# A graph layer's mean over neighbours: three sorted lanes instead of four, and keys fetched four blocks at a time

## The chip, the cores and the metric

The kernel runs on one core of a Trainium2 chip. Its engines work side by side, each through its own list of instructions in order: PE (TensorE, matrix products), DVE (VectorE), ACT (ScalarE), POOL (GpSimd, which here also issues the indirect DMAs) and SP (SyncE, which issues most plain DMAs). The time is device microseconds of one execution. A profile is one execution taken by the hardware profiler; its times are counted from the first instruction.

## The reference

```python
h = jnp.maximum(_layernorm(x, axis=-1), 0.0)
local = features[tgt]            # features = h, 100000 nodes x 64
nbr = features[src]              # 3300000 edges, sorted by tgt
x = jnp.concatenate([local, nbr - local], axis=-1)
y = jnp.einsum('ec,oc->eo', x, W) + b
s = jax.ops.segment_sum(y, tgt, num_segments=num_v)
cnt = jax.ops.segment_sum(jnp.ones((y.shape[0],), y.dtype), tgt, num_segments=num_v)
return jnp.where(cnt > 0, s / jnp.maximum(cnt, 1.0), 0.0)      # added to x
```

The layer is linear, so what costs is one sum: for each node, the rows of `h` of all its neighbours. Every node has itself as a neighbour, and about 32 others, spread over all 100,000 nodes.

## The kernel before

**Beginning.** The normalized rows are written to HBM, each as three bf16 parts whose sum is the row, with a column of ones (`h3`, 194 columns). Edges come sorted by target. Most of them are dealt out in windows of 8064 (8192 less a padding of 128), whose targets lie within 256 nodes; four windows are a quad, and a lane is the 128 partitions that hold up to 32 quads, one window a partition. There are 100 quads in lanes of 32, 32, 32 and 4. The edges that are left go in chunks of 3584 (`chunks`): one indirect DMA on POOL fetches a row of `h` for each of 128 edges, 28 of them make a chunk, and PE sums the rows with a matrix of zeros and ones that DVE makes (`hot`, L362).

**Sort** (`sort_lane`). Each partition sorts its 8192 keys by source with a bitonic network: a copy of one side (`tmp`, L481 on ACT in the first lane, L486 on POOL in the others) and a minimum and a maximum on DVE (L476, L477), with `held` letting the next copy go ahead of a compare. Sorted keys go to `ksort` in HBM. The 100,000 sources are cut into 157 blocks of 640; counts on ACT and DVE (L567, L623) tell where each block's keys begin.

**Fill** (`fill_lane`). For groups of eight blocks, `fetch` gathers 64 keys from each block's beginning with one indirect DMA per block (L672, 161 a lane). DVE splits them into source within the block and target within the window, and the results go through HBM (`sr_d`, `dt_d`) to where quads load them. Keys that fit in no block's 64 slots are spill: DVE finds up to 64 of them a window with one instruction each (L745), and one indirect DMA each fetches them (L758).

**Main part** (`quads`). A block of a quad is a "pick": `gh` (three tensor-scalar compares on DVE for eight blocks, L845) selects rows of a table of `h` by six matmuls (L873), ACT casts the result (`gs`, L875), and `dh` (a compare on DVE for four blocks, L362) sums them into the targets by sixteen small matmuls (L886). 32 blocks stay in SBUF as tables, so each lane goes over its quads in five passes of 32, 32, 32, 32 and 29 picks a quad. At the end of a quad's pass ACT copies the sums out of PSUM (L910), and in passes 1 to 4 POOL adds those of the passes before (L912). In the last pass two indirect DMAs per quad fetch spill rows (L826), and DVE then adds the nodes' own rows and joins the three parts (L919, L923, L925); SP stores the result (L342 to L345).

**Order.** Instructions are issued in the order of the Python program, which weaves its parts by an account. The sort of lane 0 runs alone with `chunks`, `own_part` and the writing of tables beside it: each step of the sort yields a number of ns, and one row gather is issued for every GATHER ns of that account. Then the fill of lane 0 makes four groups, `drain(ev)` issues the gathers that are left, and the main part begins. Beside it `background` yields the rest of the fill, the sort of the next lane and so on, in steps booked at 2.083 ns an element and 290 ns for a compare, and 480 ns for a step of the fill; each pick allows SORT ns of it. `begin`, called two groups of four blocks ahead, issues the loads of a quad; `put` issues its sums and, in the last pass, its end on DVE. `add_later` and `add_now` hand stores to SP some picks later. After the last quad come the chunks' and windows' shared rows and the last stage, the product with the weights.

The account as it stands:

```python
spent = 0.0
for _ in quads():
    spent -= SORT
    while spent <= 0:
        with pinned(last["hots"].ins):
            spent += next(rest, SORT)
```

## Time and profile before

| | before |
|---|---|
| median of 3 runs | 19243.74 us (19207.14 to 19248.48) |
| the profiled execution | 19284.92 us, its span 19283.3 us |
| first row gather, last row gather on POOL | 347 us, 1472.5 us |
| first cast of the main part | 1767.9 us |
| last cast of the main part | 18908.2 us |
| busy: PE, DVE, ACT, POOL | 82%, 76%, 48%, 24% of the span |
| mean granted TensorE clock | 0.913 of full speed |

The busy shares are averages over stages with different limits. A row of a stage names the stretch in us, its length, each engine's busy time in it with the number of instructions in brackets, the granted clock, the mean busy share of the DMA engines and the GB/s that they moved. A row of a group names line, engine, operation, what is written and read, shapes and count, then busy us and mean ns of one, then the idle time ahead of it and what ended it. A row of waits names who waited for whom, the us in total, how often, and the longest.

### The profile page before, as it was taken

The numbers are of one execution on the slowest core, as the hardware profiler recorded it, in microseconds if no ns is written. First come the engines' busy times: TensorE is split into PE (matmuls) and PEld (weight loads), VectorE is DVE, ScalarE is ACT, GpSimd is POOL, SyncE is SP. The second block draws the span as 40 slices with busy tenths as digits, with TensorE's granted clock in tenths as the row PEclk, the third lists the DMA queues.
The fourth block names the chain that finished last, engine by engine and source line by source line (L and its number), as shares of the span: only waits on it lengthen the run. The fifth ranks groups of instructions, "written<-read, shape, count | busy, mean of one in ns | idle before, by whom it ended". The sixth has DMA issues, their size and how long they took to land. (4 is left out here: it accounts for less than half of the span.)

```text
span 19283.3 us, 796285 instructions
## 1 busy us (share of the span) xinstructions
PE 15795.1 (82%) x356735; PEld 13909.3 (72%) x356735; DVE 14736.7 (76%) x17616; ACT 9286.0 (48%) x19353; POOL 4620.4 (24%) x3293
## 2 busy tenths in 40 slices
PE   0342699999998768999998877889999887898896
PEld 0332588888886557888887756778888775787785
DVE  6667579999987667899998656888889865566664
ACT  3334355555555334555556433445555643554452
POOL 6442202222222321112222231221122223111104
PEclk9556899999998789999999888999999988999998
DMA  7862334444444434344444444343344433344456
GB/s 276 121 114 75 79 115 138 126 141 127 142 122 124 101 88 119 104 132 126 143 127 134 116 101 122 100 114 104 124 121 142 118 107 102 113 134 112 121 184 238
DMA packets 1520611, 2432.07 MB, mean 126 GB/s; under 512 B 905304, under 2 KB 1113699, under 8 KB 1511011
## 3 DMA queue, kind: packets, MB, share of 16 engines
q1 hardware_dynamic: 1327762, 2081.35, 36.8%
q10 hardware_dynamic: 134086, 239.08, 4.7%
q0 software_dynamic: 55328, 60.66, 2.2%
q8 instruction: 2788, 45.68, 1.0%
q14 instruction: 647, 5.30, 0.1%
HBM read 1836.50 MB, written 583.01 MB: 125 GB/s over the span
## 5 line engine op out<-in xcount | busy, mean ns | idle before, releaser
L875 ACT CAST gs<-gp 128x386 bf16<-128x386 f32 x15700 | 7444.5, 487 | 7775.7 <-PE gp L873 7102.8
L873 PE MATMUL gp<-tab,gh 128*128 128x193 bf16 x94200 | 9142.7, 252 | 1303.1 <-ACT gs L875 460.8
L873 PEld LDWEIGHTS <-gh 128*128 128x128 bf16 x94200 | 7997.5, 99 | 2161.8 <-issue 1585.4
L886 PE MATMUL total<-gs,dh 32*128 32x193 bf16 x251200 | 6487.4, 247 | 890.1 <-issue 679.9
L886 PEld LDWEIGHTS <-dh 32*128 32x128 bf16 x251200 | 5298.9, 94 | 1823.6 <-issue 1518.4
L362 DVE TENSOR_TENSOR dh<-dt,c 128x2048 bf16<-128x2048 int16 (+1 forms) x4000 | 4737.5, 1193 | 2300.9 <-PE total L886 1771.9
L845 DVE TENSOR_SCALAR gh<-srs,pcols 128x2048 bf16<-128x2048 int16 (+1 forms) x6000 | 4976.2, 875 | 1133.4 <-PE gp L873 957.0
L486 POOL COPY tmp<-keys 128x1024 f32<-128x1024 f32 (+13 forms) x1017 | 1242.3, 1222 | 7265.2 <-DVE keys L477 6980.3
L912 POOL TENSOR_TENSOR whole<-whole,prev 128x1544 f32<-128x1544 f32 x400 | 1323.0, 3308 | 2809.9 <-ACT whole L910 2274.8
L477 DVE TENSOR_TENSOR keys<-tmp,keys 128x1024 f32<-128x1024 f32 (+10 forms) x1356 | 1838.1, 1361 | 29.3 <-issue 1.0
L476 DVE TENSOR_TENSOR keys<-tmp,keys 128x1024 f32<-128x1024 f32 (+10 forms) x1356 | 1573.4, 1165 | 315.0 <-ACT tmp L481 254.2
L910 ACT COPY whole<-total 128x386 f32<-128x386 f32 (+1 forms) x2000 | 817.4, 496 | 528.0 <-PE total L886 456.3
L672 POOL DMA_INDIRECT kf<-ksort,at_i x644 | 632.6, 982 | 1433.8 <-ACT k L713 850.1
L405 POOL DMA_INDIRECT nb<-h,si x588 | 562.3, 956 | 595.8 <-PE ps L410 283.2
L826 POOL DMA_INDIRECT rows_x<-h,xs x200 | 194.9, 975 | 1941.7 <-PE total L886 1312.4
L481 ACT COPY tmp<-keys 128x1024 f32<-128x1024 f32 (+9 forms) x339 | 338.1, 1002 | 421.5 <-issue 188.3
L994 PEld LDWEIGHTS o_ps<-w_own,hT 128*128 128x128 f32 x784 | 182.4, 287 | 445.4 <-ACT hT L988 339.3
L919 DVE SCALAR_TENSOR_TENSOR whole<-own,whole 128x193 f32<-128x193 bf16 x800 | 297.8, 413 | 138.6 <-POOL whole L912 114.6
L410 PE MATMUL ps<-nb,hot 128*128 128x193 bf16 x588 | 89.6, 327 | 361.6 <-DVE sums L423 168.3
L994 PE MATMUL o_ps<-w_own,hT 128*128 128x128 f32 x784 | 230.5, 427 | 183.5 <-ACT hT L988 136.7
L986 PE MATMUL t_ps<-ident,ht 128*128 128x128 f32 x392 | 93.3, 377 | 313.4 <-DVE keys L461 311.3
L410 PEld LDWEIGHTS <-hot 128*128 128x128 bf16 x588 | 74.2, 131 | 377.0 <-DVE sums L423 142.4
(189 smaller groups left out, 4437.9 us busy)
## 6 DMA issues: line engine op xcount, KB each, us to landing
srs<-sr_d SPq DMA_DIRECT2D x1900, 512.0 KB
part_d<-whole SPq DMA_DIRECT2D x400, 772.0 KB
prev<-part_d SPq DMA_DIRECT2D x400, 772.0 KB
tab<-tables ACTq DMA_DIRECT2D x148, 970.0 KB
ht<-hb SPq DMA_DIRECT2D x56, 896.0 KB
own<-h SPq DMA_DIRECT2D x400, 97.0 KB
tables<-h ACTq DMA_DIRECT2D x157, 242.5 KB
h<-parts SPq DMA_DIRECT2D x28, 1358.0 KB
```

Of the source, the lines that this page charges most:

```text
L362: return nc.vector.tensor_tensor(out.rearrange("p k (a d) -> p k a d", d=D), numbers[:, :, None].to_broadcast(shape), upto[:shape[0], :n]. ...
L405: last[POOL] = nc.gpsimd.indirect_dma_start(out=nb[:, j], out_offset=None, in_=h3, in_offset=bass.IndirectOffsetOnAxis(ap=si[:, u, at:at + ...
L476: nc.vector.tensor_tensor(lo, tmp, hi, ALU.min)
L477: last[DVE] = nc.vector.tensor_tensor(hi, tmp, hi, ALU.max)
L486: nc.gpsimd.tensor_copy(tmp, lo)
L672: last[POOL] = nc.gpsimd.indirect_dma_start(out=kf[:, c], out_offset=None, in_=ksort, in_offset=bass.IndirectOffsetOnAxis(ap=at_i[:, c0 + ...
L845: nc.vector.tensor_scalar(gh[:, b, :n].rearrange("p c i s -> p (c i s)"), srs[q, s // SL][:, :n].rearrange("p c i s -> p (c i s)"), pcols[ ...
L873: nc.tensor.matmul(gp[:, i], lhsT=ghots[q, s][:, b, i], rhs=row[:, b + i * (NB - NR), :CE], start=b == 0, stop=b == NR - 1)
L875: nc.scalar.copy(gs[q, s], gp)
L886: nc.tensor.matmul(total[:, i, to(b)], lhsT=hot[at, b * P:b * P + P], rhs=of[at], start=flags.get("start", False) and b == 0, stop=flags.g ...
L910: nc.scalar.copy(whole[:, i, :width], total[:, i, :width])
L912: nc.gpsimd.tensor_tensor(whole[:, :, :NT * CE], whole[:, :, :NT * CE], prevs.pop(q), ALU.add)
```

## The change

- Lanes: three of 32 quads instead of four; the padding of a window is 64 instead of 128, so a window has 8128 edges. More edges are left for the chunks. GATHER goes from 1250 to 900.
- Sort of lane 0: the compare is held back by one exchange, as in the other lanes.
- Fetch: one indirect DMA brings 320 consecutive keys from the beginning of the first of four blocks (41 a lane instead of 161). A new function, `apart_keys`, moves each of the other three blocks' keys to its place on DVE, by the bits of its distance: for each of eight bits one predicated copy. Each lane's keys in `ksort` are followed by end marks, since a fetch can run on.
- Spill: 48 slots are searched and fetched instead of 64.
- The end of a quad in the last pass is queued six picks after `put` (REST), in one go for its four windows, into one tile with two buffers; the load of the own rows comes eight picks later in the quad than before.
- SORT is 255 in the first four passes and 60 in the last; a step of the fill is booked at 500 ns.

```diff
-QUADS = 32, 32, 32, 4
+QUADS = 32, 32, 32
 LANES = len(QUADS)
 KG = 16
 JH = 14
 LAG = 3
-GATHER = 1250
-SORT = 240
+GATHER = 900
+SORT = 255, 255, 255, 255, 60
+REST = 6
 GAP = 5
 DUE = 10
 JA = 16
...
 NX = 2
-SPILL = NX * KS
-PAD = 128
+SLOTS = NX * KS
+SPILL = 48
+JOIN = 4
+BITS = 8
+FETCH = 320
+PAD = 64
 D = 4
 BIAS = 0x30000000
 END = 0x3A000000
-PIECES = 1024, 1024, 1024, 1024
+PIECES = 1024, 1024, 1024
 HEAD = 10
 COUNTS = 1
 GAIN = 2.0 ** 40
...
-    ksort = dram.tile([NL * P * WL + NT * P, 1], I32, name="ksort")
+    LONG = P * WL + NT * P
+    ksort = dram.tile([NL * LONG, 1], I32, name="ksort")
     sr_d = dram.tile([SETS, NCB, 2, P], I16, name="sr_d")
     dt_d = dram.tile([NG, P, SETS, SL * 2 * D], I16, name="dt_d")
...
             def exchange(lo, hi, tmp, *of):
+                if held and any(a < y and x < z for a, z in of for x, y in held[0][3]):
+                    compare()
                 if l == 0:
                     last[ACT] = nc.scalar.copy(tmp, lo)
-                    held.append((lo, hi, tmp, of))
-                    return compare()
-                if held and any(a < y and x < z for a, z in of for x, y in held[0][3]):
-                    compare()
-                nc.gpsimd.tensor_copy(tmp, lo)
+                else:
+                    nc.gpsimd.tensor_copy(tmp, lo)
                 compare()
                 held.append((lo, hi, tmp, of))
 
...
             row = few.tile([P, 1], F32, name="row", bufs=LANES)
-            nc.gpsimd.iota(row, pattern=[[0, 1]], base=l * P * WL, channel_multiplier=WL,
+            nc.gpsimd.iota(row, pattern=[[0, 1]], base=l * LONG, channel_multiplier=WL,
                            allow_small_or_imprecise_dtypes=True)
             at_i = few.tile([P, NCB + NO // 2], I32, name="at_i", bufs=LANES)
...
             nc.gpsimd.iota(first, pattern=[[CS, NCB]], base=BIAS >> 10, channel_multiplier=0)
+            off = piece.tile([P, NG * SL], I32, name="off", bufs=1)
+            nc.vector.memset(off.bitcast(F32), 0.0)
+            whole = NCB // JOIN * JOIN
+            joined = at_i[:, :whole].rearrange("p (h j) -> p h j", j=JOIN)
+            nc.vector.tensor_tensor(off[:, :whole].rearrange("p (h j) -> p h j", j=JOIN), joined,
+                                    joined[:, :, 0:1].to_broadcast([P, whole // JOIN, JOIN]), ALU.subtract)
+            bits = piece.tile([P, BITS, NG * SL], I32, name="bits", bufs=1)
+            for i in range(BITS):
+                nc.vector.tensor_scalar(bits[:, i], off, i, 1, op0=ALU.logical_shift_right, op1=ALU.bitwise_and)
             fetched = {}
 
+            def apart_keys(k, kf):
+
+                m = min(SL, NCB - k * SL)
+                n = m // JOIN
+                moved = piece.tile([P, SL // JOIN, JOIN - 1, FETCH], I32, name="moved", bufs=1)
+                of = kf[:, :n, None, :]
+                for i in reversed(range(BITS)):
+                    w = KW + (1 << i) - 1
+                    shape = [P, n, JOIN - 1, w]
+                    at = 1 << i
+                    if i == BITS - 1:
+                        nc.vector.tensor_copy(moved[:, :n, :, :w], of[:, :, :, :w].to_broadcast(shape))
+                        src = of[:, :, :, at:at + w].to_broadcast(shape)
+                    else:
+                        src = moved[:, :n, :, at:at + w]
+                    mask = bits[:, i, k * SL:k * SL + n * JOIN].rearrange("p (h j) -> p h j", j=JOIN)[:, :, 1:, None]
+                    nc.vector.copy_predicated(moved[:, :n, :, :w], mask.to_broadcast(shape), src)
+                    if i in (6, 4, 2):
+                        yield
+                keys = piece.tile([P, SL, KW], I32, name="keys", bufs=1)
+                to = keys[:, :n * JOIN].rearrange("p (h j) s -> p h j s", j=JOIN)
+                nc.vector.tensor_copy(to[:, :, 0], kf[:, :n, :KW])
+                if m % JOIN:
+                    nc.vector.tensor_copy(keys[:, n * JOIN], kf[:, n, :KW])
+                nc.vector.tensor_copy(to[:, :, 1:], moved[:, :n, :, :KW])
+                fetched[k] = keys
+                yield
+
             def fetch(k):
-                c0, m = (k * SL, min(SL, NCB - k * SL)) if k < NG else (NCB, NO // 2)
-                fetched[k] = kf = piece.tile([P, SL, KW], I32, name="kf", bufs=3)
-                for c in range(m):
+                fetched[k] = kf = piece.tile([P, SL // JOIN, FETCH], I32, name="kf", bufs=3)
+                starts = range(k * SL, min(k * SL + SL, NCB), JOIN) if k < NG else [NCB]
+                for h, c in enumerate(starts):
                     last[POOL] = nc.gpsimd.indirect_dma_start(
-                        out=kf[:, c], out_offset=None, in_=ksort,
-                        in_offset=bass.IndirectOffsetOnAxis(ap=at_i[:, c0 + c:c0 + c + 1], axis=0))
+                        out=kf[:, h, :NO * KS if k == NG else FETCH if c + JOIN <= NCB else KW], out_offset=None, in_=ksort,
+                        in_offset=bass.IndirectOffsetOnAxis(ap=at_i[:, c:c + 1], axis=0))
                     took()
                     yield
 
...
                 m = min(SL, NCB - c0)
+                yield from apart_keys(k, fetched[k])
                 kf = fetched.pop(k)[:, :m]
                 sr = piece.tile([P, SL, KW], I32, name="sr", bufs=1)[:, :m]
                 nc.vector.tensor_scalar(sr, kf, 10, None, op0=ALU.logical_shift_right)
...
 
-            kf = fetched.pop(NG)[:, :NO // 2]
+            kf = fetched.pop(NG)[:, 0, :NO * KS].rearrange("p (c s) -> p c s", s=KW)
             nc.vector.tensor_scalar(kf, kf, 10, None, op0=ALU.logical_shift_right)
             nc.vector.tensor_scalar(kf, kf, float(-(BIAS >> 10) - NCB * CS), float(2 * CS), op0=ALU.add, op1=ALU.min)
...
-            xpos = piece.tile([P, SPILL], F32, name="xpos", bufs=1)
+            xpos = piece.tile([P, SLOTS], F32, name="xpos", bufs=1)
             for s in range(SPILL):
                 nc.vector.scalar_tensor_tensor(more, over, float(s), fit, op0=ALU.is_le, op1=ALU.mult,
                                                accum_out=xpos[:, s:s + 1])
                 if s % 8 == 7:
                     yield
-            nc.vector.tensor_add(xpos, xpos, iota[:, :SPILL])
+            nc.vector.memset(xpos[:, SPILL:], 0.0)
+            nc.vector.tensor_add(xpos, xpos, iota[:, :SLOTS])
             nc.vector.tensor_scalar(xpos, xpos, row, None, op0=ALU.add)
-            xin = piece.tile([P, SPILL], F32, name="xin", bufs=1)
+            xin = piece.tile([P, SLOTS], F32, name="xin", bufs=1)
             nc.vector.tensor_scalar(xin, xno, -1.0, 1.0, op0=ALU.mult, op1=ALU.add)
             nc.vector.tensor_mul(xpos, xpos, xin)
-            xat = piece.tile([P, SPILL], I32, name="xat", bufs=1)
+            xat = piece.tile([P, SLOTS], I32, name="xat", bufs=1)
...
-                if k == 3 * GP:
+                if k == 5 * GP:
                     owns[q] = load.tile([P, W, NT, CT], BF16, name="own", bufs=1)
                     for i in range(W):
                         at = number(wb_r[0:1, 0, q * W + i:q * W + i + 1], SP, V)
...
                     return
+                closing.append((count[0] + REST, q, whole))
+
+            def close(q, whole):
+                sums = load.tile([P, W, NT, C1], F32, name="wsums", bufs=2)
                 for i in range(W):
                     for b in range(NT):
                         part = whole[:, i, b * CE:b * CE + CE]
                         nc.vector.scalar_tensor_tensor(part, owns[q][:, i, b, :CE], whole[:, i, NT * CE + b:NT * CE + b + 1],
                                                        part, op0=ALU.mult, op1=ALU.add)
                     both = whole[:, i, :NT * CE].rearrange("p (b c) -> p b c", b=NT)
-                    sums = load.tile([P, NT, C1], F32, name="wsums", bufs=6)
-                    nc.vector.tensor_reduce(sums[:, :, :C], both[:, :, :C3].rearrange("p b (s c) -> p b c s", s=3),
+                    nc.vector.tensor_reduce(sums[:, i, :, :C], both[:, :, :C3].rearrange("p b (s c) -> p b c s", s=3),
                                             axis=AX.X, op=ALU.add)
-                    nc.vector.tensor_copy(sums[:, :, C:], both[:, :, C3:])
-
-                    def addition(w=q * W + i, sums=sums):
+                nc.vector.tensor_copy(sums[:, :, :, C:],
+                                      whole[:, :, :NT * CE].rearrange("p w (b c) -> p w b c", b=NT)[:, :, :, C3:])
+                for i in range(W):
+                    def addition(w=q * W + i, i=i):
                         if w < SETS * W - 1:
-                            store(wb_r[0:1, 0, w:w + 1], slice(w, w + 1), [sums[:, b] for b in range(NT)])
+                            store(wb_r[0:1, 0, w:w + 1], slice(w, w + 1), [sums[:, i, b] for b in range(NT)])
                             return
                         at = number(wb_r[0:1, 0, w:w + 1], POOL, V)
-                        nc.gpsimd.dma_start(acc[ds(at, CH)].rearrange("(b p) c -> p b c", p=P), sums, accum_op=ALU.add)
+                        nc.gpsimd.dma_start(acc[ds(at, CH)].rearrange("(b p) c -> p b c", p=P), sums[:, i], accum_op=ALU.add)
 
                     add_later(DUE, addition)
 
...
-                    yield
+                for x in picks(g + 1):
+                    yield x
                     count[0] += 1
+                    while closing and closing[0][0] <= count[0]:
+                        close(*closing.pop(0)[1:])
                     add_now()
                 _, x, q, of = groups[g]
                 for s in of:
                     put(x, q, s)
+            for of in closing:
+                close(*of[1:])
 
         slots = {}
         filled = [0] * NL
...
                     for _ in fill_lane(l, fill, took):
-                        yield 2 * SORT
+                        yield 500
 
         with tc.tile_pool(name="keys", bufs=1) as big, tc.tile_pool(name="piece", bufs=2) as piece, \
...
             spent = 0.0
-            for _ in quads():
-                spent -= SORT
+            for x in quads():
+                spent -= SORT[x]
                 while spent <= 0:
                     with pinned(last["hots"].ins):
-                        spent += next(rest, SORT)
+                        spent += next(rest, 500)
             assert next(rest, None) is None
             add_now(True)
 
```

29 lines of the change are left out of this document (14 added, 15 removed).

## The prediction

> **What bounds the kernel now.** I read the page first, then the busy time of each stage, and only then the waits of single stages.
>
> ```profile
> span 19283.3 us, 796285 instructions
> PE 15795.1 (82%) x356735; PEld 13909.3 (72%) x356735; DVE 14736.7 (76%) x17616; ACT 9286.0 (48%) x19353; POOL 4620.4 (24%) x3293
> ```
>
> PE leads, but an average says little here. One ScalarE cast (`gs`, L875) closes each block ("pick"), so casts per stretch give the speed of the main part. The stretches below are its passes: lane 0 passes 0, 1+2, 3, 4; lane 1 the same; lane 2 pass 0, then passes 1 to 3 together, then 4; last, all of lane 3. Columns: stretch, length, ACT busy (casts), granted clock, DMA share, GB/s.
>
> ```profile
> 1768.00:2994.00 1226.00, 482.78 (x1024) 0.90 0.36 103
> 2994.00:4939.00 1945.00, 974.91 (x2049) 1.00 0.46 134
> 4939.00:5981.00 1042.00, 485.15 (x1024) 0.98 0.44 130
> 5981.00:7448.00 1467.00, 437.01 (x929) 0.82 0.41 101
> 7448.00:8398.00 950.00, 486.93 (x1024) 0.99 0.36 113
> 8398.00:10345.00 1947.00, 974.40 (x2049) 1.00 0.46 134
> 10345.00:11709.00 1364.00, 480.97 (x1025) 0.86 0.42 114
> 11709.00:12913.00 1204.00, 439.81 (x928) 0.90 0.42 108
> 12913.00:13863.00 950.00, 487.59 (x1024) 0.99 0.36 113
> 13863.00:17221.00 3358.00, 1456.55 (x3072) 0.94 0.41 120
> 17221.00:18286.00 1065.00, 440.63 (x931) 0.95 0.45 115
> 18286.00:18909.00 623.00, 297.67 (x628) 0.99 0.53 167
> 16440.00:17221.00 781.00, 382.45 (x804) 0.99 0.45 132
> ```
>
> A pick costs 0.925 us in a first pass (950/1024), 0.95 in passes 1 and 2 beside a sort, 0.97 with neither sort nor fill (the last row); there the clock is whole and PE sets the pace. The losses are at the ends of lanes: 1467, 1364, 1204 and 1065 us where about 930 to 980 would do. Two things lie there. One is the fill (`fill_lane`) and its gathers:
>
> ```profile
> 10820.00:11420.00 600.00, 457.60 (x8983) 378.06 (x8981) 325.39 (x467) 249.67 (x494) 197.60 (x176) 0.82 0.41 108
> 11507.00:11602.00 95.00, 24.04 (x253) 13.95 (x244) 11.15 (x17) 5.10 (x11) 64.33 (x65) 0.55 0.12 29
> L672 POOL DMA_INDIRECT kf<-ksort,at_i x157: 940/944/1292, 10819.3 to 11400.3; - x157
> ```
>
> (Columns: PE, PEld, DVE, ACT, POOL busy.) Twenty-two matmuls make a pick, so the first stretch, with 157 fetches, did 8983/22 = 408 picks in 600 us: 1.47 us each. The second holds the 64 single-key gathers of L758 in a row: 11 picks in 95 us. A long row of indirect DMAs on POOL stops PE, about 85/64 = 1.33 us for each; no engine is busy there but POOL. The other thing is the quad's end on VectorE (L919 to L925) in a last pass, seen alone in lane 2, where no background is left. First DVE's groups of 17221 to 18286, then who made PE wait there.
>
> ```profile
> L362 DVE TENSOR_TENSOR dh<-dt,c 128x2048 bf16<-128x2048 int16 (+1 forms) x257 | 286.4, 1117 | 285.3 <-DMA dt<-dt_d 150.9 <-PE total L886 95.7 <-PE gp L873 38.8
> L845 DVE TENSOR_SCALAR gh<-srs,pcols 128x2048 bf16<-128x2048 int16 (+1 forms) x387 | 272.7, 747 | 47.0 <-PE gp L873 47.0
> L919 DVE SCALAR_TENSOR_TENSOR whole<-own,whole 128x193 f32<-128x193 bf16 x248 | 92.0, 411 | 0.0
> L923 DVE TENSOR_REDUCE wsums<-whole 128x128 f32<-128x384 f32 x124 | 72.9, 588 | 0.0
> L925 DVE COPY wsums<-whole 128x2 f32<-128x2 f32 x124 | 19.4, 156 | 0.0
> ```
>
> ```profile
> PE gp L873 <- DVE gh L845: 93.2, 45, 4.0
> ```
>
> The end is 184.3 us over 31 quads, 6 us each, in one piece ahead of the next `gh`; PE waits 93 us for `gh`, 3 us a quad.
>
> **The change, part by part.** I sum against the profiled execution (1768 to the first cast, 17141 of main part, 375 of tail, 1.6 outside the span: 19284.9); the median of the runs is 41 us lower.
>
> *Three lanes.* Lane 3's 623 us go, and with them its sort and fill beside lane 2 (passes 1 to 3). Lane 2 then has no background: 0.925 x 1024 + 0.97 x 3072 = 947 + 2980.
>
> *More chunks.* 3,300,000 edges less 384 windows of 8128 leave 178,848: 50 chunks of 3584 instead of 21, 1400 row gathers instead of 588, all before the main part. Their price is the start-to-start time on POOL:
>
> ```profile
> 361.10 0.94 POOL L405 DMA_INDIRECT nb<-h,si  x1 [0.30 <-issue]
> 362.35 0.94 POOL L405 DMA_INDIRECT nb<-h,si  x1 [0.30 <-issue]
> 347.00:1473.00 1126.00, 399.25 (x2099) 329.89 (x2099) 703.73 (x717) 368.32 (x494) 561.72 (x588) 0.62 0.72 127
> 1473.00:1690.00 217.00, 8.61 (x56) 7.51 (x56) 208.28 (x298) 136.75 (x243) 0.48 (x1) 0.52 0.05 20
> 350.00:450.00 100.00, 9.02 (x32) 3.71 (x32) 43.53 (x72) 2.15 (x2) 75.10 (x78) 1.00 0.79 258
> 1350.00:1450.00 100.00, 13.92 (x84) 12.08 (x84) 99.04 (x97) 41.17 (x42) 68.35 (x73) 0.52 0.21 37
> L672 POOL DMA_INDIRECT kf<-ksort,at_i x644: 938/944/2325, 1691.9 to 16250.4; - x161
> ```
>
> So 1.25 us each. Until now the sort of lane 0 set this stage (fetches can start at 1692, gathers ended at 1473). The sort books 894 us (my sum over the numbers it yields); at 900 ns a gather 994 are woven into it, 406 are left. Woven in, the old pace of 1126/588 = 1.91 us becomes 1.91 x 0.9/1.25 = 1.38, above 1.25: hidden, but tight. In the first 100 us 77 gathers become 107 x 1.25 = 134 (+34); from 1350 to 1690, where `own_part` is over, 72 per 100 us become 100 x 1.25 = 125 (340 us, +80, less some waiting: 66). The sort ends near 1790. The 406 and the 10 fetches now needed follow with nothing beside them that POOL waits for: 520 us, to 2310, and 20 more to the first cast: 2330, **+562**. Bounds: POOL never idle from 347, 347 + 1410 x 1.25 = 2110 (+10 to the cast); above, if the sort is slowed by a third of what the woven gathers add (994 x 1.25 x 0.28 x 1/3, 116 us), 2450. SP gets 29 more stores of sums; their cover is the same stage. The other order in `exchange` of lane 0 holds the compare back one step, as the other lanes do; the copies keep their buffers, so I book nothing.
>
> *Keys four blocks per fetch.* Eight fetches a group become two: POOL's row of 10 us, which starved PE, becomes 2.5, and two gathers in a row I book at nothing for PE (if they stopped it as the long rows do, 2 x 1.33 us in each of 60 groups, 160 in all). In their place DVE gets eight predicated copies of 6 x (64 + 2^i - 1) elements, 4554 in all, and copies of 1658. The trace has predicated copies of other sizes, and an int32 pass of 512:
>
> ```profile
> L464 DVE COPY_PREDICATED s<-own,q 128x512 int32<-128x512 int32 x60 | 44.3, 738 | 8.4 <-remote 3.3 <-issue 2.8 <-DVE q L463 1.0
> L701 DVE COPY_PREDICATED kf<-far,kf 128x256 int32<-128x256 int32 x76 | 36.9, 485 | 0.0
> L694 DVE TENSOR_SCALAR sr<-kf 128x512 int32<-128x512 int32 x76 | 31.9, 420 | 27.2 <-issue 15.5 <-DMA kf<-ksort,at_i 11.8
> L362 DVE TENSOR_TENSOR dh<-dt,c 128x2048 bf16<-128x2048 int16 x3900 | 4696.2, 1213 | 2278.2 <-PE total L886 1749.2 <-remote 230.2 <-DMA dt<-dt_d 217.5
> L745 DVE SCALAR_TENSOR_TENSOR more<-over,fit 128x314 f32<-128x314 f32 x256 | 124.2, 485 | 6.8
> L745 DVE DVE_READ_ACCUMULATOR more<-over,fit 128x1 f32 x256 | 21.2, 83 | 0.0
> L438 DVE TENSOR_REDUCE wb<-keys 128x1 f32<-128x8064 int32 x4 | 34.2, 8553 | 68.2 <-DMA keys<-in_dst_w 68.2
> L623 DVE TENSOR_SCALAR_CACHE_REDUCE junk<-keys 128x534 bf16<-128x534 f32 x152 | 106.9, 704 | 2.0
> ```
>
> From 485 and 738: 0.99 ns an element and 0.23 fixed, 4.5 + 1.9 = 6.4 us; copies at 0.82 ns, 1.3: 7.7 us a group. Bounds: nothing if DVE's idle time took it all, twice that if broadcast operands run at half rate; I take the middle, the shapes being alike. The fill's old DVE work is (325.4 - 408 x 0.583)/18 = 4.9 us a group, 0.583 being three `gh` (747) and two `dh` (1213) per eight picks. A group books nine steps of 500, 4.5 us, which is 17.6 picks at 255 and 75 at 60. At 255 DVE needs 17.6 x 0.583 + 12.6 = 22.9 us for 17.6 picks: 1.30 us a pick, **DVE becomes the bound of the fill**, 6.6 us lost per group. Before, (600 - 408 x 0.925)/18.4 = 12.1. By the account 16 groups fall into lane 0's first pass, 11 into its pass 3, 9 into pass 4 at 60 (covered, 20 us in all), and lane 2's 20 into lane 1's pass 3. The scan of 48 spill steps (L745, 0.57 us each, 27 us against twelve picks' time of which DVE needs 7) costs 23 us, the 48 gathers 48 x 1.33 = 64 where they run in a row (lane 0's first pass), 50 between the quads' additions of a pass 3, little in pass 4.
>
> The Trainium skill, "SBUF — State Buffer", section "SBUF: two separate sides", speaks against this part: an fp32 copy within SBUF on VectorE locks GpSimd out, so a DMA issued there takes about 3.1 us instead of 0.62. By it the two fetches of a group would cost an estimated 4 us more; the fill's rows show 944 ns at the median beside such DVE work.
>
> *Pace.* 255 instead of 240 beside a sort is 6% more sort, on a DVE that is 92% busy beside one:
>
> ```profile
> 8500.00:9300.00 800.00, 774.53 (x18494) 692.24 (x18493) 738.97 (x701) 438.85 (x945) 192.95 (x113) 1.00 0.45 128
> ```
>
> Of its 739 us 249 are not one-hots (840 picks at 0.583); 6% of them are 15, two in a hundred of the stretch, most of it idle time. I take 0.956 for 0.950.
>
> *The end six picks later, 60 in the last pass.* Behind two more `dh` and the next eight blocks' `gh`, the 6 us run when PE has about two groups of four in hand (7 us): the 93 us go. DVE holds 743 us of the rows above over 32 quads, 23 each and one `eh`, against PE's 29 x 0.925 = 27 and the end's small matmuls. A last pass becomes 1065 - 93 - about 40 of lower clock = 930, and 950 in lane 0 with nine groups beside it. The own rows' load is queued two groups later on SP, behind the end that must free `own`; both move together, so the `srs` and `dt` loads behind it see the same wait.
>
> *The sum.* Lane 0: 947 + 16 x 6.6 + 23 + 64 + 27 (a sort's start, unchanged: the two reductions of 8.55 us and part of the 17 us that their load is waited for) = 1166; 2048 x 0.956 = 1957; 979 + 50 (VectorE's 70 counts at 0.70 in one piece, unchanged) + 73 = 1102; 950. Lane 1: 983; 1959; 979 + 50 + 132 + 23 + 50 = 1234; 930. Lane 2: 947 + 2980 + 930. Together 5175 + 5106 + 4857 = 15138 against 17141: -2003. With +562: 19284.9 - 1441 = 17844, less 41: **17,800**.
>
> **Rivals.** *The gathers hide* (12%): the sort loses nothing and POOL stays full to 2120: 17,590. For it: POOL is idle half of 347 to 1473; against: 406 gathers have no sort left. *DVE takes the fill in its idle time* (6%): -47 x 6.6: 17,490; against it the 92%. *The masks run at half rate* (11%): 47 x 7.7 more: 18,160. *The late end buys nothing* (10%), because `gh` is late for another reason (its `srs` load, or the `dt` that DVE waited 151 us for): three last passes at 1065, 18,205. *Fetches wait for VectorE* (2%): each at the longest time seen, 2325 ns, 47 x 2.8 = 130: 17,930; this is what the skill's page would make of it, and the median speaks against it. *Slower* (3%): the predicated copies with a stride-zero mask cost not 0.99 but over 7.7 ns an element. Then the 47 groups at full pace take 31 us more each, 1441 in all, and at 8.5 ns it ends near 19,400. No row shows such a rate; the two at hand are both near 1.
>
> **How the numbers follow.** The forecast has 56%, its own range 17,600 to 18,000. With the rivals next to it the range is 17,450 to 18,250. A measurement of this kernel tells about 0.2% (its runs lie 19207 to 19248) from no change; every case but the last is far beyond it: faster 0.96, same 0.01, slower 0.03.
>
> **What would show it.** First cast near 2330 with POOL nearly full from 1400 on; lane 2's passes near 0.93 and 0.97 a pick; a fill with DVE above 95% and about 1.3 us a pick, no stretch where only POOL is busy in pass 3 of 157 fetches; last passes near 930 with PE's wait on `gh` gone. A first cast before 2150 or after 2450, or last passes above 1000, would prove the step wrong.

## The result and the profile after

The changed kernel takes 18557.48 us (median of four runs, 18551 to 18577); the kernel before takes 19235.75 beside it. The ratio is 0.9651, interval 0.9634 to 0.9668: 678 us faster, where 17,800 was forecast, outside the range of 17,450 to 18,250. The profiled execution is 18577.3, its span 18575.7. The engines' line of its page:

```profile
PE 15064.2 (81%) x343411; PEld 13353.6 (72%) x343411; DVE 13652.2 (73%) x16240; ACT 8851.9 (48%) x18429; POOL 4303.4 (23%) x3101
```

The busy time of each stage, lane 0's passes 0, 1+2 and 4; lane 1's 1+2, 3 and 4; lane 2's pass 0, its passes 1 to 3 and its pass 4. The last row is a piece of lane 1's pass 3 in which the fill runs. (Columns: stretch, length, PE, PEld, DVE, ACT, POOL busy with instructions, granted clock, DMA share, GB/s.)

```profile
2574.00:3738.00 1164.00, 992.02 (x22415) 873.62 (x22417) 949.11 (x1325) 566.98 (x1182) 136.70 (x128) 0.92 0.37 110
3738.00:5688.00 1950.00, 1886.28 (x45081) 1688.90 (x45077) 1847.37 (x1739) 1069.87 (x2305) 494.01 (x292) 1.00 0.46 134
6808.00:8008.00 1200.00, 965.61 (x22985) 840.59 (x22986) 860.59 (x1415) 510.50 (x1077) 221.44 (x153) 0.90 0.42 109
8987.00:10933.00 1946.00, 1884.26 (x45040) 1687.93 (x45032) 1830.50 (x1732) 1070.04 (x2304) 482.69 (x289) 1.00 0.46 134
10933.00:12210.00 1277.00, 1032.56 (x22544) 899.98 (x22536) 1013.28 (x1470) 640.13 (x1369) 235.85 (x153) 0.90 0.44 122
12210.00:13297.00 1087.00, 945.75 (x23003) 832.10 (x22992) 714.47 (x1078) 489.41 (x1056) 161.46 (x94) 0.93 0.41 113
13297.00:14244.00 947.00, 934.08 (x22544) 841.71 (x22545) 571.62 (x651) 534.76 (x1152) 5.10 (x3) 0.99 0.35 113
14244.00:17142.00 2898.00, 2817.10 (x67580) 2527.21 (x67572) 1879.56 (x1921) 1604.78 (x3456) 302.54 (x95) 1.00 0.45 135
17142.00:18201.00 1059.00, 930.53 (x22928) 819.25 (x22920) 706.40 (x1070) 489.32 (x1056) 159.57 (x92) 0.95 0.40 108
11455.00:11890.00 435.00, 328.09 (x6691) 280.89 (x6693) 389.09 (x589) 194.35 (x374) 71.49 (x47) 0.86 0.45 123
```

Against the forecast's terms: first cast 2574 for 2330 (+244); lane 0's last pass 1200 for 950 (+250), lane 1's 1087 for 930 (+157), lane 2's 1059 for 930 (+129); lane 1's pass 3 1277 for 1234 (+43); lane 2's passes 1 to 3 2898 for 2980 (-82). The others are within 18. The sum is +733, which is the whole miss. Lane 2's last pass took 1065 before, some 24 of it in its last quad, where lane 3 began (1.93 us a pick, 1.11 now): the late end bought it nothing.

Two stages stand out by their waits. First that of lane 0's sort (347 to 2070), then lane 2's last pass (17142 to 18201; SPq is SP's own queue). Columns: who waits, for whom, us in total, times, longest.

```profile
ACT tmp L489 <- issue: 264.9, 78, 41.5
```

```profile
DVE dh L368 <- DMA dt<-dt_d: 207.4, 26, 11.9
PE gp L917 <- DVE gh L889: 110.7, 55, 3.8
...
SPq L348 <- DMA acc<-wsums: 301.1, 120, 3.5
SPq L351 <- DMA acc<-wsums: 74.9, 76, 2.6
```

In the first, ACT's copies for the sort stand up to 41.5 us at "issue", waiting for nothing that the profile shows. In the second, DVE waits for `dt` and PE for `gh` as before. SP stands 376 us at the stores of window sums, each of which waits for the store before it to land.

### The profile page after: what moved, and what is told of

Same layout as the page of the kernel before. It is cut to its first block, busy times and chain, and to the rows that moved or that the text cites. A ratio compares the mean times of both kernels' runs of the same rounds, so it can differ in the third digit from the quotient of the medians.

```text
span 18575.7 us, 764868 instructions
## 1 busy us (share of the span) xinstructions
PE 15064.2 (81%) x343411; PEld 13353.6 (72%) x343411; DVE 13652.2 (73%) x16240; ACT 8851.9 (48%) x18429; POOL 4303.4 (23%) x3101
## 5 line engine op out<-in xcount | busy, mean ns | idle before, releaser
L919 ACT CAST gs<-gp 128x386 bf16<-128x386 f32 x15072 | 7152.7, 487 | 7033.2 <-PE gp L917 6204.4
L917 PE MATMUL gp<-tab,gh 128*128 128x193 bf16 x90432 | 8669.7, 250 | 805.7 <-ACT gs L919 357.1
L917 PEld LDWEIGHTS <-gh 128*128 128x128 bf16 x90432 | 7603.4, 99 | 1593.2 <-issue 1065.4
L930 PE MATMUL total<-gs,dh 32*128 32x193 bf16 x241152 | 6082.0, 246 | 509.0 <-issue 315.6
L930 PEld LDWEIGHTS <-dh 32*128 32x128 bf16 x241152 | 5043.4, 94 | 1305.5 <-issue 1057.3
L889 DVE TENSOR_SCALAR gh<-srs,pcols 128x2048 bf16<-128x2048 int16 (+1 forms) x5760 | 4694.0, 861 | 1043.4 <-PE gp L917 1027.0
L491 POOL COPY tmp<-keys 128x1024 f32<-128x1024 f32 (+11 forms) x678 | 828.4, 1223 | 4588.4 <-DVE keys L483 4311.6
L482 DVE TENSOR_TENSOR keys<-tmp,keys 128x1024 f32<-128x1024 f32 (+13 forms) x1017 | 1189.1, 1176 | 501.8 <-ACT tmp L489 322.3
L411 POOL DMA_INDIRECT nb<-h,si x1400 | 1339.8, 957 | 856.8 <-issue 437.2
L483 DVE TENSOR_TENSOR keys<-tmp,keys 128x1024 f32<-128x1024 f32 (+13 forms) x1017 | 1360.6, 1346 | 20.4 <-DVE q L469 1.0
L713 POOL DMA_INDIRECT kf<-ksort,at_i x123 | 134.0, 1089 | 912.6 <-DVE keys L702 782.8
```

What stands on the lines that cost most here:

```text
L411: last[POOL] = nc.gpsimd.indirect_dma_start(out=nb[:, j], out_offset=None, in_=h3, in_offset=bass.IndirectOffsetOnAxis(ap=si[:, u, at:at + ...
L482: nc.vector.tensor_tensor(lo, tmp, hi, ALU.min)
L483: last[DVE] = nc.vector.tensor_tensor(hi, tmp, hi, ALU.max)
L491: nc.gpsimd.tensor_copy(tmp, lo)
L889: nc.vector.tensor_scalar(gh[:, b, :n].rearrange("p c i s -> p (c i s)"), srs[q, s // SL][:, :n].rearrange("p c i s -> p (c i s)"), pcols[ ...
L917: nc.tensor.matmul(gp[:, i], lhsT=ghots[q, s][:, b, i], rhs=row[:, b + i * (NB - NR), :CE], start=b == 0, stop=b == NR - 1)
```

## Experiments

### The first stage: what a row gather costs the sort

The theories: the forecast's (woven gathers hide until POOL is full); that gathers hold up the other engines; that chunk work in the in-order engines does; and that lane 0's new exchange order does.

**No weaving.** `-GATHER = 900` `+GATHER = 10 ** 9`

> One constant of the changed kernel, GATHER, from 900 to 10**9: no row gather is woven into lane 0's sort, all 1400 follow it. In the changed kernel the sort ended at 2069 (the first fetch of keys) with 994 woven, before at 1692 with 588. Forecast's theory (the sort goes at its own pace, a woven gather costs it nothing or a third of what POOL adds): sort end 1650 to 1700, first cast near 1690 + 1400 x 1.25 + 33 = 3470. Rival (each woven gather stops the sort's engines for about (2069 - 1692)/(994 - 588) = 0.93 us): 2069 - 994 x 0.93 = 1145, but DVE alone has some 910 us of work from 347 on, so 1260 to 1350; first cast near 3080. Second rival (the other order in lane 0's exchange slows the sort): sort end near 2000, first cast near 3800. In the stretch of the sort DVE should then be above 0.85 busy by the first rival only.

**Gathers alone.** The loop of `chunks` without its one-hot, matmuls, sums and stores:

```
-                    with behind():
-                        one_hot(hot, near[:, u, part * JH:part * JH + JH], P)
...
-                    before = (hot, nb, part, q)
+                    before = None
```

> Leaves out of the chunks' part the one-hot, the matmuls, the sums and their stores; the 1400 row gathers stay, 994 of them woven into the sort as in the changed kernel. If the gathers themselves hold up the other engines: the sort still ends at 1920 to 2070, and while POOL issues gathers back to back DVE and ACT stand still although nothing in the sort waits for the gathers. If the sort was held up by its in-order engines waiting for chunk work (hot for PE, ps for the sums): 1690 or earlier. The main part is not touched: last passes as in the changed kernel (1200, 1087, 1059).

**Chunks without gathers.** Matmuls read one tile of zeros: `+nb = still`, and the indirect DMA is removed.

> The counterpart: the row gathers are left out (the matmuls read one tile of zeros), and the chunks' one-hots, matmuls, sums and stores stay, in the same places of the program. If the gathers hold up the engines: the sort ends at 1400 or earlier with DVE above 0.85 busy. If the chunk work holds it up: 1900 or later. First cast soon after the sort's end, since only the last 406 places of chunk work without a gather are left.

**Gathers with a long pause**, on gathers alone: `+last[POOL] = nc.gpsimd.memset(still, 0.0)` with `still` 128x1400, ordered behind each gather and ahead of the next.

> As the run with the gathers alone (chunk one-hots, matmuls, sums and stores left out, 1400 row gathers kept), with one POOL memset of 128x1400 floats behind every gather, about 1.25 us, which needs nothing and is needed by nothing. Gathers alone, the sort ended at 2909 and did nearly nothing while POOL issued every 1.25 to 1.4 us. If it is the unbroken row of gathers that stops the other engines: gathers come every 2.5 us and last to about 3850, and yet the sort ends at 1750 or earlier, DVE being busy between 500 and 1500 as without any gather (70 to 95 us in 100). If each gather takes a fixed time from the others, whatever lies between: half the time is left to them, the sort ends near 347 + 2 x (1474 - 347) = 2600.

The stretch 500 to 1400 (columns as above) in four kernels, in this order: changed; gathers alone; with pauses; chunks without gathers.

```profile
500.00:1400.00 900.00, 342.76 (x1836) 285.38 (x1836) 477.47 (x461) 278.89 (x386) 485.14 (x513) 0.58 0.72 121
```

```profile
500.00:1400.00 900.00, 71.82 (x295) 57.08 (x294) 108.65 (x97) 72.04 (x92) 680.62 (x648) 0.50 0.30 54
```

```profile
500.00:1400.00 900.00, 290.62 (x1398) 235.54 (x1395) 715.09 (x642) 405.68 (x535) 839.27 (x754) 0.55 0.73 115
```

```profile
500.00:1400.00 900.00, 353.10 (x2092) 299.37 (x2091) 774.15 (x760) 410.30 (x556) 0.00 (x0) 0.62 0.63 93
```

The 87 counts on ACT that end the sort (min/median/max ns, first to last start), for the three experiments in the same order (chunks without gathers last):

```profile
L569 ACT ACTIVATE junk<-keys,bound x87: 501/742/743, 2822.9 to 2906.3; 128x536 bf16<-128x536 f32 x58, 128x430 bf16<-128x430 f32 x22, 128x258 bf16<-128x258 f32 x7
```

```profile
L571 ACT ACTIVATE junk<-keys,bound x87: 501/742/743, 1370.7 to 1453.9; 128x536 bf16<-128x536 f32 x58, 128x430 bf16<-128x430 f32 x22, 128x258 bf16<-128x258 f32 x7
```

```profile
L573 ACT ACTIVATE junk<-keys,bound x87: 500/742/743, 1390.8 to 1474.3; 128x536 bf16<-128x536 f32 x58, 128x430 bf16<-128x430 f32 x22, 128x258 bf16<-128x258 f32 x7
```

Without gathers the sort ends at 1474, with one every 2.39 us (the median; its memset takes 1.28) at 1454. With POOL left to issue as fast as it can, one every 1.25 us, it ends at 2906, and DVE is busy 109 us of 900, with nothing else of the chunks' work there. The unbroken row is the cause; whether the break between two gathers counts or their rate, which it halves, is not separated. Chunk work and the exchange order are not the cause: the run without gathers keeps both. One stop and its end, in the timeline of the gathers alone (start, duration, engine; in brackets the idle time before):

```profile
1585.96 1.22 DVE L480 TENSOR_TENSOR keys<-tmp,keys 128x1024 f32<-128x1024 f32 x1
...
1598.49 0.95 POOL L408 DMA_INDIRECT nb<-h,si  x1 [0.30 <-issue]
1599.45 0.37 ACT L1045 COPY own<-o_ps 128x256 f32<-128x256 f32 x1 [14.78 <-remote]
...
1599.88 0.27 PE L1042 MATMUL o_ps<-b,ones 96*128 96x128 bf16 x1 [13.78 <-issue]
1600.77 1.22 DVE L479 TENSOR_TENSOR keys<-tmp,keys 128x1024 f32<-128x1024 f32 x1 [13.59 <-issue]
```

DVE, ACT and PE stop together for some 14 us, while POOL issues every 1.25, and go on together.

My rival's figure of 0.93 us a gather was no constant. Without weaving the sort ended at 2640 instead of 1260 to 1350 and the first cast came at 2695: POOL ran the gathers ahead all the same, 1400 between 346 and 2518, since nothing in its list held them back. It also failed for the gathers alone, which ended 840 us later than its upper figure: with no chunk work, nothing breaks the row. What the changed kernel loses depends on how often POOL has to wait.

**A short pause** behind each gather of the complete kernel, as above with `still` 128x28.

> The changed kernel, complete, with a POOL memset of 128x28 floats (0.15 us for 128x56 bf16 in the stage ahead) behind each of the 1400 row gathers. If a short break is enough for the others to go on: the sort ends near 1700 to 1850 instead of 2069, and the first cast comes near that + 400 x 1.45 = 2300 to 2400. If it is POOL's share of time that counts: sort unchanged near 2069, the row behind it 10% longer, first cast 2620 to 2680.

The sort ended at 1980 instead of 2021, the first cast came at 2597 instead of 2574, the whole took 18575.6. But the memset made no break in the row:

```profile
2199.67 0.95 POOL L413 DMA_INDIRECT nb<-h,si  x1 [0.17 <-issue]
2200.61 0.15 POOL L417 MEMSET still<- 128x28 f32 x1
2200.93 0.95 POOL L413 DMA_INDIRECT nb<-h,si  x1 [0.17 <-issue]
```

It falls into the 0.30 us that POOL stands idle ahead of each gather anyway, and the gathers come every 1.25 us (the median) as in the changed kernel. So the run says nothing of a short break. How far apart gathers must be, between 1.25 and 2.39 us, was not tried.

### The last passes

**The end at once.** `-closing.append((count[0] + REST, q, whole))` `+close(q, whole)`

> The changed kernel with the quad's end on VectorE queued where it was before (directly behind the copies of the sums), nothing else undone. Forecast's theory (the end's 6 us ahead of gh are what PE waits for, 93 us a last pass): the three last passes become about 93 us longer each, 1290, 1180 and 1150, the kernel 18830. Rival on record (the late end buys nothing, gh is late for another reason): last passes 1200, 1087 and 1059 within 20 each, the kernel within 60 of 18557.

18556.4, with last passes of 1181, 1085 and 1067. The waits of its lane 2's last pass:

```profile
DVE dh L368 <- DMA dt<-dt_d: 208.5, 51, 6.3
...
PE gp L917 <- DVE gh L889: 114.0, 57, 3.8
```

The same totals as with the late end, in twice as many waits for `dt`. The six picks of delay move the wait, and do not shorten it.

**No window stores** into `acc` in the last passes (`if len(tiles) == 1:` ahead of them).

> The changed kernel without the two stores of each window's sums into acc in the last passes (the one shared row is still stored; the chunks' stores stay). In the changed kernel SP's queue waited 301 + 75 us at these stores in lane 2's last pass, each for the one before it to land, and DVE waited 190 us for dt, whose load is queued on SP behind them. If that is what makes gh late: DVE's wait for dt is below 40, the last passes go from 1200, 1087 and 1059 to 1060, 950 and 930 (15 each), the kernel to some 18150. If gh is late because DVE is too full in a last pass (dh, gh, eh and the end): last passes within 20 of before, the kernel 18500 or more.

18310.8 for this kernel, which leaves those sums out. Lane 2's last pass, and its wait for `gh`:

```profile
16974.00:17952.00 978.00, 912.93 (x22957) 808.02 (x22952) 773.26 (x1071) 490.30 (x1057) 159.87 (x92) 0.97 0.37 109
```

```profile
PE gp L916 <- DVE gh L888: 56.5, 32, 2.1
```

DVE waits for no `dt` any more, PE half as long for `gh`, and the last passes are 1111, 984 and 978: 89, 103 and 81 less. So the stores cost some 90 us in each. The remaining 978 is 48 above my 930. That sum had taken off all of PE's 93 us of waiting for `gh`, and 56 of them are still there; why `gh` is still late was not followed further. ("The end's small matmuls" are no part of the miss: they take 37 us here and took 38 in the 1065 from which the forecast started.)

Three complete kernels tried to take the stores out of the way.

**Loads ahead**: `+loads(g + AHEAD)` with `AHEAD = 4`, the loads of `srs` and `dt` taken out of `begin(g + 2)`.

> The changed kernel, complete, with the srs and dt loads of a group issued four groups ahead instead of two (the other loads stay two ahead; buffers unchanged at three). If late loads behind SP's stores are the cause: DVE's wait for dt in lane 2's last pass falls from 190 to below 60, the last passes to 1090, 980 and 950 (20 each), the kernel to some 18230. If the stores take so much of SP's time that a longer lead only moves the wait: within 60 of 18557.

18713.7: slower by 156, last passes 1237, 1142 and 1106. SP stands longer still at the stores, 415 us in lane 2's last pass where it was 376, and DVE's wait for `dt` stays (215 us between 17250 and 18250, 201 in the changed kernel). The loads had three buffers as before. With four, the kernel did not fit in SBUF (8 KB a partition asked, 5.125 left), so whether the buffers hold the longer lead back is not shown.

**dt pinned**: `+last[SP] =` at the load of `dt`, so that the stores called for later are ordered behind it too.

> The changed kernel with one word more: the load of dt, not that of srs, is remembered as SP's last, so that the stores of a window are ordered behind both. In the changed kernel the stores slipped in between: in lane 2's last pass srs was issued at 17500.05 and its dt at 17507.92, behind two stores that each waited for the one before. If that order is the cause: DVE's wait for dt in the last pass of lane 2 falls from 190 to below 40, the last passes to 1110 to 1130, 985 to 1010 and 975 to 1000 where they were 1200, 1087 and 1059; some 250 less in all. If SP is short of time altogether, the wait goes to srs and gh, and the last passes stay within 25.

18211.7 beside 18117.5 for the changed kernel on the same chip; last passes 1216, 1127 and 1106, there 1184, 1084 and 1068. DVE's wait for `dt` between 16750 and 17700 only fell from 190 to 166: a store of the window before still came between. Ordering the later stores behind `dt` does not help.

**Stores by POOL**: `queue = nc.sync if by == SP else nc.gpsimd` in `store`.

> The changed kernel with each window's three stores of the last passes issued by POOL instead of SP, behind the same waits and in the same order among themselves; the chunks' stores stay on SP. If it is SP's queue, held by stores that wait for one another, that makes the loads of dt late: DVE's wait for dt goes as in the run without stores (none above 20 us in all), the last passes to 1115, 990 and 985 (15 each), the kernel to some 18300. If it is the stores' traffic or their landing themselves: no gain, 18557 within 60. If POOL is late with them (it stands in order behind fetches and row gathers): wsums runs out of buffers, the last passes above 1100 in lanes 1 and 2.

Its last passes are 1260, 1180 and 1167, the slowest of all. The waits of the last one:

```profile
POOL acc L352 <- DMA acc<-wsums: 274.8, 90, 4.4
POOL acc L349 <- DMA acc<-wsums: 233.1, 120, 4.8
DVE whole L968 <- POOL whole L957: 231.5, 30, 11.8
```

DVE's wait for `dt` is gone from this list, as in the run without stores: SP's queue, held by the stores, is what makes `dt` late. But the chain of stores that wait for one another goes along to POOL, where the addition of the passes' sums (L957) now stands behind it, and DVE's end behind that. The third case of its expectation came out; the whole took 18393.7, where the changed kernel takes 18117.5 on a chip of that kind (below). No remedy was found: in both queues the stores wait for one another, and what stands behind them waits too. Stores that need not wait for one another were not tried.

### The joined fetch, on chips where rows of gathers stop nothing

The last two sets of runs met other chips, on which the kernel before takes 18411.8 and 18405.2 us instead of 19217 to 19247.

**The changed kernel again**, unchanged.

> The changed kernel itself, for its trace on this call's chip. If the chip is like the first ones: 18557 within 40 beside 19235 of the kernel before, first cast 2574. If it is like that of the third set (before at 18412): first cast near 2207, the quad with the 48 gathers 1.3 to 2 us a pick, the whole about 18080.

It took 18117.5 beside 18405.2: 288 us faster there, not 678. The first cast comes at 2212 with the same instructions. What differs can be seen in the row of 48 key gathers of lane 1's spill, first the result's trace, then this one:

```profile
11990.00:12052.00 62.00, 15.69 (x129) 8.15 (x129) 8.11 (x10) 2.41 (x5) 48.11 (x48) 0.53 0.17 44
```

```profile
11550.00:11613.00 63.00, 32.49 (x711) 28.45 (x712) 18.99 (x23) 16.75 (x36) 49.11 (x48) 0.74 0.23 60
```

With the same 48 gathers PE does 711 matmuls instead of 129. In the row of lane 0's first pass it does 1398 in 61 us, the full pace of 23 a us, where the result's trace has 122 in 59. What is left of a price on these chips comes from POOL's list being in order: in lane 1's row the addition of the passes' sums stands behind most of the 48 gathers, SP waits 44.9 us for it at the load of `prev`, and DVE 39.0 us for the `dt` whose load is queued behind that. In lane 0's last pass the addition stands behind all 48, the quad's end on DVE waits 51.5 us for it, and the quad still takes 2.80 us a pick. And while lane 0 is sorted DVE is busy 656 us of 500 to 1400, with more gathers issued:

```profile
500.00:1400.00 900.00, 384.60 (x2034) 301.22 (x2033) 656.16 (x640) 352.41 (x468) 624.46 (x662) 0.60 0.80 130
```

**Old fetch**: the changed kernel with `fetch` as before and without `apart_keys`.

> The changed kernel with the joined fetch undone: eight fetches of 64 keys per group in place of two of 320, and none of the masked copies that take them apart. If the forecast's account of the fill holds (before 12.1 us lost a group, joined 6.6): lane 1's pass 3 becomes 20 x 5.5 = 110 us longer, 1390, lane 0's first pass 90 longer, 1250. By the changed kernel's own fill (304 picks in 435 us, 1.43 a pick, 10 us lost a group) the gain is only some 2 us a group: 1317 and 1196, the kernel 100 longer, 18660. If the masked copies cost VectorE as much as the fetches cost PE: the same within 30.

**Lanes only**: the kernel before with `QUADS = 32, 32, 32`, three `PIECES`, `PAD = 64` and `GATHER = 900`.

> The kernel before with three lanes, windows 64 longer and GATHER 900, and nothing else of the change (single fetches, exchange order, pace and end as they were). By the sum of the forecast with its parts taken out: on a chip where rows of gathers stop the others, lane 0's first pass 90 and lane 1's pass 3 some 110 longer than with the joined fetch, hence 18700 to 18800; if the joined fetch is worth nothing, 18500 to 18600. On a chip like that of the third set, where undoing the joined fetch gained: about 17900.

**dt pinned, old fetch, all woven** (`GATHER = 640`).

> The changed kernel with dt pinned, with single fetches again (no masked copies), and with all row gathers woven into lane 0's sort. By stage: last passes as in dt_pinned. The joined fetch's worth stands in lane 0's first pass and lane 1's pass 3 (1164 and 1277 with it): on a chip where rows of gathers stop the others I expect 1250 and 1390 if the forecast's account holds, the same within 30 if the masked copies cost what the fetches cost; on a chip like the third set's 1032 and 1106 as there. First cast: 2440 on the former kind of chip, 2210 on the latter. In all 18250 on the former, 17650 on the latter.

17878.3, 17980.5 and 17986.3; the last has a ratio of 0.9776 to before, interval 0.976 to 0.9793. (It is 108 above the old fetch: its last passes, dt pinned, are some 130 longer together, and its first cast at 2227 gains 9.) The last had been expected at 17650, with the gain that pinning `dt` did not bring. The expectation for the old fetch was written for chips of the result's kind. All three runs met chips of the second kind. Three fences follow: the changed kernel (lane 0's pass 0, lane 1's passes 3 and 4, lane 2's last pass), the old fetch (the same without lane 2's), the lanes alone (lane 0's pass 0, lane 1's pass 3, lane 2's last pass).

```profile
2212.00:3315.00 1103.00, 976.05 (x22428) 869.52 (x22430) 949.17 (x1324) 567.45 (x1182) 139.40 (x128) 0.94 0.40 116
10492.00:11740.00 1248.00, 1022.53 (x22512) 900.75 (x22508) 1011.58 (x1469) 640.61 (x1368) 237.05 (x153) 0.89 0.45 125
11740.00:12824.00 1084.00, 946.63 (x23005) 833.11 (x22994) 714.87 (x1078) 489.53 (x1056) 161.27 (x94) 0.93 0.42 113
16673.00:17741.00 1068.00, 939.00 (x22988) 826.84 (x22984) 707.57 (x1071) 490.02 (x1057) 159.35 (x92) 0.94 0.40 108
```

```profile
2236.00:3268.00 1032.00, 948.38 (x22418) 849.23 (x22416) 824.16 (x1137) 567.82 (x1182) 211.98 (x206) 0.98 0.43 124
10344.00:11450.00 1106.00, 987.47 (x22554) 875.67 (x22548) 866.01 (x1127) 637.38 (x1363) 319.59 (x238) 0.95 0.48 138
11450.00:12597.00 1147.00, 948.52 (x22998) 833.66 (x22987) 754.56 (x1228) 492.09 (x1062) 210.72 (x143) 0.92 0.42 108
```

```profile
2236.00:3283.00 1047.00, 954.28 (x22433) 852.29 (x22435) 809.89 (x1148) 567.74 (x1182) 216.36 (x206) 0.97 0.42 122
10504.00:11679.00 1175.00, 985.18 (x22532) 874.30 (x22528) 855.75 (x1244) 640.61 (x1367) 356.93 (x280) 0.93 0.47 131
16578.00:17608.00 1030.00, 923.00 (x22956) 815.54 (x22948) 720.85 (x1163) 490.45 (x1056) 159.67 (x92) 0.96 0.43 111
```

On these chips the joined fetch is a loss: 71 us in lane 0's pass 0, 142 in lane 1's pass 3, and 239 in all (18117.5 - 17878.3, one run each, on two chips whose kernel before differs by 7). Of the 142, 63 come back in the next pass (1147 against 1084): there the old fetch has its row of spill gathers, which in the changed kernel stands in pass 3. It takes 125 us of DVE's time in pass 0 (949 against 824), and there is no stop of PE to be saved. The lanes alone, with their padding and GATHER, give 425 of before's 18405; the rest of the change takes 137 back. Not only the fetch does: lane 2's last pass, where no fill is left, takes 1030 with before's end and 1068 with the change's. SP stands 384 us at the stores there instead of 307, and DVE 194 for `dt` instead of 169. Which part of the new end (one go, one tile with two buffers, the later load of own rows) does that was not tried. The old fetch within the changed kernel is the fastest seen on such chips, 17878.3, single. Whether the joined fetch gains where rows stop the others was not measured by itself; by the rows alone a fill group lost 12.1 us before and 8.8 in the result, at different paces.

**Paused spill, all woven**: the memset of 128x1400 behind each of the 48 spill gathers, and `GATHER = 640`.

> Two edits of the changed kernel that touch different stages. (1) Behind each of the 48 gathers of spilled keys a POOL memset of 128x1400 floats, 1.25 us, so that they come every 2.5 us instead of in an unbroken row. If the unbroken row stops PE: the three quads that held it (3.35, 3.53 and 3.12 us a pick) go below 1.6, some 60 us each, 180 in all. If each gather costs PE its 1.3 us wherever it stands: 48 x 1.3 us stay, spread over four quads each, nothing won. (2) GATHER 640 in place of 900: all 1400 row gathers woven into lane 0's sort. By the slope of the runs so far (a woven gather delays the sort 0.8 to 0.95 us, one behind it costs 1.25 to 1.3): first cast 2574 - 330 x 0.4 = 2440 (2400 to 2500). If what is woven closer only makes rows that are unbroken: 2574 or later, as in the run without weaving (2695).

It met a chip of this kind too, where neither has a stop to remove: the first cast came at 2204, and lane 0's pass 0 was 1146 instead of 1103, since DVE waits longer for the last key. 18152 us; on the chips of the result it is untried.

## Why the prediction was wrong, by its steps

**Three lanes** held: 623 us of lane 3 went, lane 2's pass 0 took 947 for 947, its passes 1 to 3 ran at 0.943 a pick instead of 0.97 (82 us better; why is open).

**More chunks** is the first step that failed. "Woven in ... above 1.25: hidden, but tight" counted POOL's time, and a gather's price on the other engines as nothing. On the chips of the result an unbroken row stops the other engines, and at 900 the woven gathers were such rows: the sort ended at 2021 instead of 1790, the first cast came 244 late, beyond the upper bound of 2450. That bound had let the sort slow down by a third of what the woven gathers add; the rows had to be read for what the other engines did meanwhile. The quoted row of 64 gathers in 95 us showed it ("A long row of indirect DMAs on POOL stops PE"), and I used it for the spill alone. Where rows stop nothing, 2212 was even ahead of the 2330.

**Joined fetch.** The account was of the right kind and too low. 304 picks (6691/22) in 435 us are 1.43 us each for 1.30, 8.8 us lost a group (154/17.5) for 6.6; over the 20 groups of lane 1's pass 3 the 43 us of its miss. DVE's work was not the term too low: (389 - 304 x 0.583)/17.5 = 12.1 us a group, booked at 12.6. But the account let DVE never wait, and it was busy 89%, not above 95: there it waits 35 us of the 435 for PE. A stop by the two gathers is not behind it, since those quads take 1.41 us a pick on both kinds of chip. Lane 0's pass 0 came out as forecast (1164 for 1166) by luck: the trace has 27 fetches in it, some 13.5 groups instead of 16, each losing more. The masked copies' widest, 1146 elements, took 1.46 us for 1.37 (min/median/max ns, first to last start; the fetches above them):

```profile
L713 POOL DMA_INDIRECT kf<-ksort,at_i x123: 943/1050/1705, 2069.1 to 11894.5; - x123
...
L697 DVE COPY_PREDICATED moved<-bits,kf x60: 800/1460/4395, 2076.8 to 11933.6; 128x1146 int32<-128x1146 int32 x57, 128x573 int32<-128x573 int32 x3
```

A fetch takes 1.05 us at the median, 0.1 more than before. The figure of 3.1 us that the Trainium skill, "SBUF — State Buffer", section "SBUF: two separate sides", gives for a DMA issued by GpSimd beside a copy on VectorE is not reached in that row, whose longest is 1.7: the 77 fetches that ran beside these copies took 1.06 at the median. The page states it for an fp32 copy, and these are int32, most of them masked.

**The end six picks later** is the second step that failed: "the 93 us go". PE's wait for `gh` was 111 us after the change, and with the end at once 114, in a kernel of the same time. The rival "the late end buys nothing, because `gh` is late for another reason (... the `dt` that DVE waited 151 us for)" was right, 10% and 18,205. Its row stood in the quoted fence of DVE's groups; I had read 151 us as idle time of an engine with room, though DVE's list is in order and the next `gh` stands behind the `dh` that waits. The stores on SP are behind some 90 us of the 129 that lane 2's last pass was late. Lane 1's missed 28 more, about what its last quad loses at 2.05 us a pick, where lane 2 begins. Lane 0's last pass has two misses more: its spill row came in one piece (a quad at about 3.5 us a pick, where 29 picks lose some 67 us against the pass's usual 1.2), though I had booked "little in pass 4", and the fill groups "covered" at 20 us (13 fetches, some six groups instead of nine); with lane 2's 129 and the 67 taken off, some 50 us of its 250 are left for those.

**Pace** (1950 and 1946 for 1957 and 1959) held, and so did the tail.

## What to carry to other kernels

Price an instruction that goes in a long unbroken row by what the other engines do while the row runs, not by its own engine's free time; a row seen earlier in the same trace may say it. When an engine that works in order waits for a load, ask what stands behind that wait before moving work around it, and whose queue the load stands in. A pause put between two instructions has to be looked up in the trace: the short memset here filled idle time and spread nothing. And a trade of one engine's time for another's stall has to be measured on more than one chip: here it may pay on one and costs 239 us on another.

## What the runs showed of the hardware

On some chips (before at 19217 to 19247 us) indirect DMAs issued back to back by POOL, 1.25 us apart, stop PE, DVE and ACT together for 10 us and more at a time; 2.39 us apart, with 1.28 us of other work on POOL between them, they stop nothing. On two other chips (before at 18405 to 18412) the same instructions at the same spacing stop PE and DVE hardly at all (1398 matmuls beside a row of 48 gathers, 122 on the first kind). The two kinds differ by 440 us on the changed kernel, of which 362 lie before the first cast and 61 in lane 0's pass 0. On the kernel before they differ by some 830, more than the change itself is worth; how much of that is the stops was not traced. What differs between the chips is not known; each set of runs met one chip at one time, so that it is the chip itself is not shown either. The width of the data does not decide it: the 48 gathers of one key a partition stop PE as those of whole rows of `h` do.

The Trainium skill, "Runtime: NRT & Kernel Launch", section "Instruction fetch mechanics", says that engines fetch instructions in blocks of 16 KiB, 256 instructions, through DMA queues of their own, mostly hidden. A late fetch would fit engines that wait for nothing else, but the row of the DMA queues for the gathers alone, 500 to 1400, doesn't show that these blocks are slow to move:

```profile
q14 instruction: 7, 0.06, 0.0%
q8 instruction: 2, 0.03, 0.0%
```

Nine packets took no share of the time that could be read. And the engines stop more often than a block ends: PE did 295 matmuls in those 900 us and stood still 37 times for over 8 us. Whether a block is asked for late can't be seen here; the mechanism stays open.
